# Issuing transposed strips from one queue, and writing out the order at the end of self attention, in a one-core Perceiver block

## The chip, the cores and the metric

The kernel runs on one core of one Trainium2 chip. Its metric is device time in microseconds, which is the time of one launch. In the profile the engines are PE (TensorE, matmuls; PEld is its weight load), DVE (VectorE), ACT (ScalarE), POOL (GpSimd) and SP (SyncE, which issues DMAs). A name with a q behind it (SPq, ACTq) is the engine's queue issuing a DMA.

## What is computed

The input is 8 rows of 128 tokens with 512 features, and 8 contexts of 2048 tokens with 384 features, all in float32. Cut to its core, the reference is:

```python
x = x + cross_attention(layernorm(x), ctx)  # 8 heads of 64, 2048 keys, then Wo and bo
x = x + self_attention(layernorm(x))        # 1 head of 512, causal mask, over 128 tokens
                                            # returns minibatch + read; softmax over axis 1
x = x + ffn(layernorm(x))                   # 512 -> 2048 (relu, rounded to e4m3), w2 rounded
                                            # to e4m3, -> 512, b2 and the output to e5m10
```

The "row" of this text is one of the 8 batch rows, a tile of 128 x 512.

## The kernel before

**Cross attention** is a loop over 8 batches `b`, and in it over 4 steps `m` of two heads each. In a step, `scores(b, m)` multiplies queries and keys (tile `sc`, line 568), and VectorE copies the products into the tile `p` with the maxima as a by-product (line 572). `p` lies in a pool with a single buffer. `exps` takes the exponential of both heads on ScalarE (line 586), after all maxima are there. `turns` transposes `p` in 32x32 blocks on VectorE (line 599), and 16 DMAs, the *strips* (line 605), move the blocks to their places in `pT`. In the next step, `attend` multiplies `pT` with the values (tile `po`, line 617). Between them TensorE works through a *unit*, which is one part of the next batch's key or value projection (lines 469 and 492). A unit is a generator: its results leave PSUM by copies on ScalarE (`take`) and additions on VectorE, and it yields three times, so that other instructions can be placed between its parts.

Of the strips, SyncE's queue gets the first 12 (`STRIPS[:-Q]`, `Q` is 4). The last four go to ScalarE's queue, behind the first two or three parts of the unit. In the last batch, from step 1 on, three queues share the 16.

**Row transfers** go from ScalarE's queue at the start of a step, right behind `scores` in program order. Step 1 has `load_u` (a constant line, line 658). Step 3 stores two tiles of the batch before (`xtd` and `xr`, lines 906 and 907) and loads the next row (`load_x`, line 654). SyncE's queue also carries the context loads of `next_half` (line 190, at steps 0 and 3) and `load_q` (line 550, at step 0).

**Self attention** is split into two groups of four rows, `sa0` and `sa1`. Their methods are `norm`, `turn` (transpose on TensorE, copy by ScalarE into `xt`), `keys` (`psk`, copied to `sk` by ScalarE), `weights` (logits `pl`, exponential), `probabilities`, `values` (`psv`) and `read` (`pr`). The first group runs inside the last batch's steps 1 to 3. The second comes after the loop, mixed with the last `attend` and the last two projects (`py`). Then the feed forward begins: `hidden` (`ph`), `output` (`pf`), and `quantize_w2`, which rounds `w2` in 16 chunks on ScalarE and VectorE.

**What sets the order.** Each engine's instructions of a `manual_schedule` block stand in the order of the program text. TensorE is under such a block through the whole kernel. ScalarE (`in_turn`) and VectorE (`first`) are so until `first.close()` and `in_turn.close()`. What is written after that is placed by a planner, and in the trace some of it stands between the instructions of the blocks (square roots of the feed forward's norms, rounding of `w2`). PSUM gives seven banks to all tiles that are made by `bank`.

Of the kernel before, what the change touches and what calls it, by code (L numbers as in the profile page):

```python
# [17 lines left out]
P = 128  # L18
# [49 lines left out]
def tile_perceiver_block(  # L68
# [75 lines left out]
    def normed(b, pool, tag, bufs, name, add_to=False):  # L144
        xn = pool.tile([P, D], F32, tag=tag, name=f"xn_{name}_{b}", bufs=bufs)
        normed_into(xn, b, name)
        if add_to:
            nc.gpsimd.tensor_tensor(xs[b], xs[b], xn, ALU.add)
        return xn
# [219 lines left out]
    wv_sums = wxa.tile([P, len(WSLOT), 256], F32, tag="wv_sums", name="wv_sums")  # L369
    sum_w(lambda k, j: wk4[:, k, :, j, :], wk_sums, nc.vector)  # L370

    kts, vts, ps_, sums, qts, turned_, pos, nms, wides = [{} for _ in range(9)]

    def block_product(name, mm, views, outs):

# [177 lines left out]
    def scores(b, m):  # L553

        q = qts[b][:, m, :]
        if m == 0:
            sums[b] = small.tile([P, NH], F32, tag="sums", name=f"sums_{b}")
        mx = small.tile([P, 2, NJ], F32, tag="mx", name=f"mx_{b}_{m}", bufs=3)  # L560

        home, tag = (ktp, "kt0") if (b, m) == (B - 1, 2) else (pp, "p")
        p = home.tile([P, Q, 2, J // Q], F32, tag=tag, name=f"p_{b}_{m}")
        for n in range(NJ):
            pair = [bank(f"sc_{b}_{2 * m + i}_{n}") for i in range(2)]
            for i in range(2):
                r = slice(i * DH, (i + 1) * DH)
                nc.tensor.matmul(  # L568
                    pair[i], q[r, :], kts[b, m // 2][r, m % 2, ts(n, 512)], start=True, stop=True
                )  # L570
            for i in range(2):
                nc.vector.tensor_scalar(  # L572
                    p[:, :, i].rearrange("p g (t i) -> p t g i", i=SQ)[:, ts(n, Q)],
                    pair[i].rearrange("p (t g i) -> p t g i", g=Q, i=SQ),
                    1.0, None, ALU.mult, ALU.max, accum_out=mx[:, i, n : n + 1],
                )
        top = small.tile([P, 2], F32, tag="top", name=f"top_{b}_{m}", bufs=3)
        nc.vector.reduce_max(top, mx, axis=AX.X)
        nm = small.tile([P, 2], F32, tag="nm", name=f"nm_{b}_{m}", bufs=3)
        nc.vector.tensor_scalar(nm, top, -SCALE, None, ALU.mult)  # L580
        ps_[b, m], nms[b, m] = p, nm

    def exps(b, m, i):

        p, h = ps_[b, m], 2 * m + i
        nc.scalar.activation(  # L586
            p[:, :, i], p[:, :, i], AF.Exp, bias=nms[b, m][:, i : i + 1], scale=SCALE,
            accum_out=sums[b][:, h : h + 1],
        )
# [137 lines left out]
    class SelfAttention:  # L727


        def __init__(self, g, pool, w):  # L730
# [6 lines left out]
            self.vals = pool.tile([P, GB, D], F32, tag="sv", name=f"sv_{g}")  # L737
            self.xn, self.es = {}, {}

        def norm(self, b):  # L740
            self.xn[b] = normed(b, self.pool, "xn", GB, "s", add_to=True)
            unread = self.pool.tile([P, D], BF16, tag="unread", name=f"unread_{b}")
            row_constant(b, self.xn[b], self.u, unread)

# [62 lines left out]
                self.values(r)  # L807
            yield

        def values_and_reads(self, rows):  # L810
            for r in rows:
                self.values(r)
            for r in self.rows:
                self.read(r)
            yield

        def read(self, b):
            ps = bank(f"pr_{b}")
# [75 lines left out]

    sa0 = None
    for b in range(B):
        last = b + 1 == B
        for m in range(NK):  # L900
            scores(b, m)

            if m == 1 and b > 0 and not last:
                load_u(b - 1)
            if m == 3 and b > 0 and not last:
                nc.scalar.dma_start(xtd[:, :, ts(b - 1, S)], stats[b - 1])
                nc.scalar.dma_start(xr[:, b - 1, :], xs[b - 1])
            if m == 3 and b < B - 2:
                load_x(b)
            unit = None  # L910
            if m > 0:
                attend(b, m - 1)
            elif b > 0:

                attend(b - 1, NK - 1)
            if m == 0:
                unit = v_proj(b, 1)
            elif not last and m == 1:
                unit = v_proj(b + 1, 0)
            elif not last:  # L920
                unit = k_proj(b + 1, m - 2)
            elif m == 1:
                unit = sa0.keys(sa0.rows)
            elif m == 2:
                unit = sa0.weights_and_values(sa0.rows[:3])
            else:
                unit = sa0.values_and_reads(sa0.rows[3:])
            if b == m == 0:

                keys = k_proj(0, 1, (1,))  # L930
                first_of(keys)
                first_of(keys)
                exps(b, m, 0)
                all_of(keys)
            else:
                exps(b, m, 0)
                if unit and not (last and m > 0):
                    first_of(unit)
            if m == 3 and last:
                bring_rows()  # L940
                for r in sa0.rows:
                    sa0.probabilities(r)
            exps(b, m, 1)
            if b == m == 0:
                all_of(both_weights())
            if m == 0 and b > 0:
                turned = normalized_first(b - 1)
                if last:
                    bring_last_rows()
            if m == 1 and b > 0 and not last:  # L950
                row_stats(b - 1)
            if m == 2 and b > 0 and not last:
                norm_rows(b - 1)
            strips = turns(b, m)
            if last and m > 0:

                strips([nc.sync, nc.gpsimd, nc.scalar], STRIPS)
            else:
                strips([nc.sync], STRIPS[:-Q])
            if m == 0 and b > 0:  # L960
                ot = normalized(b - 1, turned)
            if m == NK - 1:
                inverse_sums(b)
            if not (last and m > 0):

                for _ in range(3 if b == m == 0 else 2):
                    first_of(unit)
                strips([nc.scalar], STRIPS[-Q:])
            if unit:
                all_of(unit)  # L970
            if m == 1 and b > 0 and not last:
                row_scale(b - 1)
            if m == 3:
                next_half(b + 2, 0)
            if m == 0:
                next_half(b + 1, 1)
                if not last:
                    load_q(b + 1)
                if b > 0:
                    project(b - 1, ot)  # L980
                if last:
                    sap, w, sa0 = enter_self_attention()
    sa1 = SelfAttention(1, sap, w)
    sa1.norm(B - 2)
    for r in sa1.rows[:2]:
        sa1.values(r)
    sa1.turn(B - 2)
    attend(B - 1, NK - 1)
    ot = normalized(B - 1, normalized_first(B - 1))
    sa1.values(B - 2)  # L990
    xa.close()
    project(B - 1, ot)
    sa1.norm(B - 1)
    keys = first_of(sa1.keys(sa1.rows[:3]))

    sa1.turn(B - 1)
    all_of(keys)
    sa1.values(B - 1)
    all_of(sa1.keys(sa1.rows[3:]))
    first.close()  # L1000
    in_turn.close()

# [12 lines left out]
    def quantize_w2():  # L1015
        quantize(nc, tp, b2q, b2r, E5M10, "qb")
        for c in range(NHC):
# [2 lines left out]
            up = tp.tile([P, D], BF16, tag="w2c", name=f"w2c_{c}")  # L1020
            nc.scalar.activation(up, w, AF.Abs, scale=UP)
            round_e4m3(nc, tp, w2[:, c, :], w, up, "qw")

    def normed_rows(g, tag):
        xt = sap.tile([P, NK, GT], F32, tag=tag, name=f"xf_{g}")
        for b in range(g * GB, (g + 1) * GB):
            turned_into(xt, b, normed(b, sap, "xn", GB, "f"), "f")
        return xt

    hqs, firsts = {}, {}  # L1030

# [33 lines left out]

    def finish(b, ps, cols=slice(0, D), add=nc.gpsimd):
        n = cols.stop - cols.start
        y = sap.tile([P, n], F32, tag="xn", name=f"y_{b}_{cols.start}", bufs=GB)
        nc.vector.tensor_tensor(y, ps[:, cols], b2q[:, cols], ALU.add)  # L1069
        quantize(nc, tp, y, y, E5M10, "qb")  # L1070
        add.tensor_tensor(y, y, xs[b][:, cols], ALU.add)
        nc.sync.dma_start(out[b][:, cols], y)

    for r in sa1.rows:
        sa1.weights(r)
    for r in sa1.rows:
        sa1.probabilities(r)
    xf0 = normed_rows(0, "xt0")
    for r in sa1.rows:
        sa1.read(r)  # L1080
    quantize_w2()
    half, xfs = NHC // 2, [xf0]
    pairs = [range(b, b + 2) for b in range(0, B, 2)]
    hidden(pairs[0], xf0, range(0, NHC, 4))
    for i in range(1, len(pairs)):
        last = i + 1 == len(pairs)
        if i == 1:
            xfs.append(normed_rows(1, "xt1"))
        hidden(pairs[i], xfs[i // 2], range(0, half, 4))
        for b in pairs[i - 1]:  # L1090
            ps = bank(f"pf_{b}")
            output(b, ps, range(NHC))
            finish(b, ps)
        hidden(pairs[i], xfs[i // 2], range(half, NHC - 4 if last else NHC, 4))
# [58 lines left out]
```

## Time and profile before

| What | Value |
|---|---|
| Median of 3 runs | 1111.77 us (1110.84 to 1111.8) |
| The profiled execution | 1111.72 us |
| Its span, first to last instruction | 1109.9 us |
| TensorE clock granted | 0.998 |
| Cross attention's first `scores` | 84.26 us |
| Last `scores` of the loop | 899.56 us |
| First `ph` of the feed forward | 962.19 us |
| Last matmul | ends at 1098.99 us |

A line of the timeline has start, duration, engine, source line, operation, the written tile and the tiles read, and how many instructions it merges. In brackets stands the idle time ahead of it and what ended it. A line of the waits has the waiting engine and tile, what it waited for, the total, the number of times and the longest, in us.

### The profile page before, as it was taken

Reading aid. Unit: us, or ns where it says so; the run is one execution under the profiler, and the core shown is the slowest. Engines: PE = TensorE matmul, PEld = TensorE weight load, DVE = VectorE, ACT = ScalarE, POOL = GpSimd, SP = SyncE. Lnnn points to the kernel's source line nnn. Section 1 sums busy time; section 2 is a strip of 40 time slices with the busy share of each in tenths; the row PEclk is TensorE's granted clock in tenths of the full one; section 3 lists DMA queues with packets and bytes.
Section 4 is the critical chain, followed back from the end, with each engine's and each line's share of the span. In section 5 each row is a group of like instructions: output and inputs, shape, how many; then the busy total and the mean of one; then the engine's idle time right before and its main releaser. Section 6 shows DMA issues by size and latency. Waiting matters only on the chain. (4 is left out here: it accounts for less than half of the span.)

```text
span 1109.9 us, 17006 instructions
## 1 busy us (share of the span) xinstructions
PE 1096.2 (99%) x6286; PEld 830.7 (75%) x6286; DVE 811.0 (73%) x1736; ACT 381.8 (34%) x627; POOL 239.2 (22%) x349
## 2 busy tenths in 40 slices
PE   9999999999999999999999999999999999999997
PEld 5485888878787777878788878887777645787775
DVE  5975577778777776877787777777876575986656
ACT  3322233324233323333243324233323322663332
POOL 0244130440044005401520450044001011000001
PEclk9999999999999999999999999999999999999999
DMA  9376234544455445344534554555436457400001
GB/s 324 130 190 166 91 77 109 156 136 100 124 147 142 105 116 170 77 114 134 142 76 115 154 139 99 134 155 130 104 77 186 137 162 246 112 3 20 16 4 39
DMA packets 71859, 134.85 MB, mean 121 GB/s; under 512 B 28240, under 2 KB 36448, under 8 KB 70752
## 3 DMA queue, kind: packets, MB, share of 16 engines
q1 hardware_dynamic: 55264, 97.03, 32.5%
q10 hardware_dynamic: 13632, 26.88, 8.8%
q0 software_dynamic: 2880, 9.85, 2.7%
q8 instruction: 50, 0.82, 0.3%
q14 instruction: 33, 0.27, 0.1%
HBM read 54.01 MB, written 10.49 MB: 58 GB/s over the span
## 5 line engine op out<-in xcount | busy, mean ns | idle before, releaser
L586 ACT ACTIVATE p<-p,nm 128x2048 f32<-128x2048 f32 x64 | 128.2, 2003 | 411.9 <-DVE nm L580 370.6
L599 DVE STREAM_TRANSPOSE p<-p 128x512 f32<-128x512 f32 x256 | 158.9, 679 | 61.1 <-ACT p L586 60.8
L572 DVE TENSOR_SCALAR_CACHE_REDUCE p<-sc 128x512 f32<-128x512 f32 x256 | 159.0, 687 | 28.5 <-PE sc L568 18.2
L229 POOL TENSOR_TENSOR m<-x 128x256 f32<-128x256 f32 x70 | 51.2, 732 | 500.5 <-DMA x<-in_ctx_t_dram 362.7
L492 PE MATMUL pv_z<-wv_sums,x 128*128 128x256 f32 x640 | 157.9, 381 | 0.0
L469 PE MATMUL pk_z<-x,wk_sums 128*128 128x256 f32 x600 | 149.9, 382 | 0.7 <-ACT kt L388 0.6
L492 PEld LDWEIGHTS pv_z<-wv_sums,x 128*128 128x128 f32 x640 | 120.4, 190 | 18.6 <-issue 2.9
L617 PEld LDWEIGHTS po<-pT,v 128*64 128x64 f32 x2048 | 111.1, 137 | 23.7 <-issue 22.1
L469 PEld LDWEIGHTS pk_z<-x,wk_sums 128*128 128x128 f32 x600 | 112.4, 190 | 20.4 <-DVE xn_s L681 1.0
L568 PE MATMUL sc<-kt,q 64*128 64x512 f32 x512 | 122.7, 603 | 1.0 <-DVE p L572 1.0
L617 PE MATMUL po<-pT,v 128*64 128x128 f32 x2048 | 118.9, 274 | 0.0
L1049 PE MATMUL ph<-xf,w 128*128 128x256 f32 x512 | 111.3, 379 | 0.0
L1049 PEld LDWEIGHTS ph<-xf,w 128*128 128x128 f32 x512 | 97.2, 190 | 13.9 <-issue 0.5
L492 PE MATMUL pv_z<-wv_sums,m 128*128 128x256 f32 x448 | 107.3, 379 | 0.0
L469 PE MATMUL pk_z<-m,wk_sums 128*128 128x256 f32 x420 | 101.4, 379 | 0.0
L568 PEld LDWEIGHTS sc<-kt,q 64*128 64x128 f32 x512 | 48.2, 186 | 63.4 <-issue 55.4
L492 PEld LDWEIGHTS pv_z<-wv_sums,m 128*128 128x128 f32 x448 | 83.4, 190 | 12.6 <-POOL x L229 0.6
L469 PEld LDWEIGHTS pk_z<-m,wk_sums 128*128 128x128 f32 x420 | 78.4, 190 | 11.8 <-DVE kt L391 0.4
L388 ACT COPY v<-pv_z 128x512 f32<-128x512 f32 x112 | 63.0, 590 | 56.7 <-PE pv_z L492 56.7
L388 ACT COPY kt<-pk_z 128x512 f32<-128x512 f32 (+1 forms) x112 | 59.9, 563 | 55.8 <-PE pk_z L469 55.4
L229 POOL TENSOR_TENSOR x<-x 128x256 f32<-128x256 f32 x98 | 70.2, 736 | 0.6 <-DMA x<-in_ctx_t_dram 0.5
L391 DVE TENSOR_TENSOR v<-pv_z,v 128x512 f32<-128x512 f32 x96 | 63.1, 685 | 5.5 <-PE pv_z L492 5.5
(200 smaller groups left out, 1258.1 us busy)
## 6 DMA issues: line engine op xcount, KB each, us to landing
pT<-p SPq DMA_DIRECT2D x366, 128.0 KB, 2.4
x<-in_ctx_t_dram SPq DMA_DIRECT2D x45, 512.0 KB, 5.6
pT<-p ACTq DMA_DIRECT2D x131, 128.0 KB, 3.0
w<-in_w_t_dram SPq DMA_DIRECT2D x1, 4096.0 KB, 13.8
w2f<-in_w_t_dram SPq DMA_DIRECT2D x16, 256.0 KB, 2.7
x_in<-in_x_dram SPq DMA_DIRECT2D x8, 256.0 KB, 7.0
qd<-xq SPq DMA_DIRECT2D x8, 256.0 KB, 2.5
q<-qd SPq DMA_DIRECT2D x8, 256.0 KB, 3.2
```

What stands on the lines that cost most here:

```text
L229: eng.tensor_tensor(x_block(b, h, to), x_block(b, h, one), x_block(b, h, two), ALU.add if op == "+" else ALU.subtract,)
L388: nc.scalar.copy(outs[ij], views(ps))
L391: nc.vector.tensor_tensor(outs[to], views(ps), outs[other], op)
L469: nc.tensor.matmul(ps[:, ts(i, BK)], wk_sums[:, WSLOT[WAT[r]], f2, :], x_block(b, h, XAT[r]), start=start and i == 0, stop=True, skip_grou ...
L492: nc.tensor.matmul(ps[:, ts(t, 256)], x[:, ts(t, P)], wv_sums[:, WSLOT[WAT[r]], :], start=start and t == 0, stop=True, skip_group_check=True,)
L568: nc.tensor.matmul(pair[i], q[r, :], kts[b, m // 2][r, m % 2, ts(n, 512)], start=True, stop=True)
L572: nc.vector.tensor_scalar(p[:, :, i].rearrange("p g (t i) -> p t g i", i=SQ)[:, ts(n, Q)], pair[i].rearrange("p (t g i) -> p t g i", g=Q, ...
L586: nc.scalar.activation(p[:, :, i], p[:, :, i], AF.Exp, bias=nms[b, m][:, i : i + 1], scale=SCALE, accum_out=sums[b][:, h : h + 1],)
L599: nc.vector.transpose(p[:, g, i], p[:, g, i])
L617: nc.tensor.matmul(pos[b][h * DH : (h + 1) * DH, ts(m, P)].rearrange("p (a i) -> p a i", a=Q), v[:, jt % 8, ts(2 * m + h, DH)], turned_[b, ...
L1049: nc.tensor.matmul(ps[:, :n], w1[:, k, ts(c, P)], xt[:, k, at], start=(k == 0), stop=(k == NK - 1),)
```

## The change

It has two parts.

First, the strips of regular steps: all 16 now go to SyncE's queue, and the four on ScalarE's are gone. A new function `after_strips` puts a small copy on ScalarE at steps 1 and 3, ahead of the row transfers. The copy reads one of the maxima that VectorE makes with its first copy of the new `p`.

Second, the end of self attention. `norm` is split into `stats` (VectorE), `scale` (square root on ScalarE) and the rest. The values of the fourth row of `sa0` and its reads move out of step 3 to behind the loop. The norms of the feed forward's first four rows, an exponential of a constant (`warm`), the second group's weights, probabilities and reads, and the transposes of the feed forward's first group now stand inside the written order, with the last row's weights and probabilities behind those of the three rows before it. The blocks are closed after that.

```diff
-        ps_[b, m], nms[b, m] = p, nm
+        ps_[b, m], nms[b, m], mxs[b, m] = p, nm, mx
+    def after_strips(b, m):
+        seen = small.tile([P, 1], F32, tag="seen", name=f"seen_{b}_{m}")
+        nc.scalar.copy(seen, mxs[b, m][:, 0, 0:1])
...
+        def stats(self, b):
+            st = small.tile([P, 6], F32, tag="st", name=f"st_s_{b}", bufs=4)
+            nc.vector.bn_stats(st, xs[b])
+            mv = small.tile([P, 2], F32, tag="mv", name=f"mv_s_{b}", bufs=4)
+            nc.vector.bn_aggr(mv, st)
+            self.xn[b] = (mv,)
+        def scale(self, b):
+            sd = small.tile([P, 1], F32, tag="sd", name=f"sd_s_{b}", bufs=4)
+            nc.scalar.activation(sd, self.xn[b][0][:, 1:2], AF.Sqrt, bias=eps)
+            self.xn[b] += (sd,)
         def norm(self, b):
-            self.xn[b] = normed(b, self.pool, "xn", GB, "s", add_to=True)
+            mv, sd = self.xn[b]
+            rs = small.tile([P, 1], F32, tag="rs", name=f"rs_s_{b}", bufs=4)
+            nc.vector.reciprocal(rs, sd)
+            self.xn[b] = self.pool.tile([P, D], F32, tag="xn", name=f"xn_s_{b}", bufs=GB + 2)
+            nc.vector.tensor_scalar(self.xn[b], xs[b], mv[:, 0:1], rs, ALU.subtract, ALU.mult)
+            nc.gpsimd.tensor_tensor(xs[b], xs[b], self.xn[b], ALU.add)
             unread = self.pool.tile([P, D], BF16, tag="unread", name=f"unread_{b}")
             row_constant(b, self.xn[b], self.u, unread)
...
+    def turned_rows(g, rows, tag):
+        xt = sap.tile([P, NK, GT], F32, tag=tag, name=f"xf_{g}")
+        for i, xn in enumerate(rows):
+            turned_into(xt, g * GB + i, xn, "f")
+        return xt
...
             scores(b, m)
+            if m % 2 and not last:
+                after_strips(b, m)
             if m == 1 and b > 0 and not last:
                 load_u(b - 1)
...
             else:
-                unit = sa0.values_and_reads(sa0.rows[3:])
+                sa1 = SelfAttention(1, sap, w)
...
                 for r in sa0.rows:
                     sa0.probabilities(r)
+                sa1.stats(B - 2)
             exps(b, m, 1)
+            if m == 3 and last:
+                sa1.scale(B - 2)
...
             else:
-                strips([nc.sync], STRIPS[:-Q])
+                strips([nc.sync], STRIPS)
...
-            if not (last and m > 0):
-                for _ in range(3 if b == m == 0 else 2):
-                    first_of(unit)
-                strips([nc.scalar], STRIPS[-Q:])
             if unit:
                 all_of(unit)
...
-    sa1 = SelfAttention(1, sap, w)
+    sa0.values(sa0.rows[-1])
     sa1.norm(B - 2)
     for r in sa1.rows[:2]:
         sa1.values(r)
+    sa0.reads()
     sa1.turn(B - 2)
     attend(B - 1, NK - 1)
     ot = normalized(B - 1, normalized_first(B - 1))
     sa1.values(B - 2)
     xa.close()
     project(B - 1, ot)
+    sa1.stats(B - 1)
+    sa1.scale(B - 1)
     sa1.norm(B - 1)
+    xf0 = [normed(b, sap, "xn", GB + 2, "f") for b in range(GB)]
+    nc.scalar.activation(warm, eps, AF.Exp)
     keys = first_of(sa1.keys(sa1.rows[:3]))
     sa1.turn(B - 1)
     all_of(keys)
     sa1.values(B - 1)
+    for r in sa1.rows[:3]:
+        sa1.weights(r)
+    for r in sa1.rows[:3]:
+        sa1.probabilities(r)
     all_of(sa1.keys(sa1.rows[3:]))
+    sa1.weights(B - 1)
+    xfs = [turned_rows(0, xf0, "xt0")]
+    sa1.probabilities(B - 1)
+    sa1.reads()
     first.close()
     in_turn.close()
...
-    for r in sa1.rows:
-        sa1.weights(r)
-    for r in sa1.rows:
-        sa1.probabilities(r)
-    xf0 = normed_rows(0, "xt0")
-    for r in sa1.rows:
-        sa1.read(r)
     quantize_w2()
```

The feed forward's second group of norms and transposes keeps its place and is written with the new helper; the tiles `xn` and `y` get six buffers instead of four.

More of the change, by code (lines that the diff above doesn't have):

```diff
@@ L370, in tile_perceiver_block @@
     sum_w(lambda k, j: wk4[:, k, :, j, :], wk_sums, nc.vector)
-    kts, vts, ps_, sums, qts, turned_, pos, nms, wides = [{} for _ in range(9)]
+    kts, vts, ps_, sums, qts, turned_, pos, nms, wides, mxs = [
+        {} for _ in range(10)
+    ]
     def block_product(name, mm, views, outs):
@@ L808, in weights_and_values, with reads @@
             yield
-        def values_and_reads(self, rows):
-            for r in rows:
-                self.values(r)
+        def reads(self):
             for r in self.rows:
                 self.read(r)
-            yield
         def read(self, b):
@@ L1022, in quantize_w2 @@
             round_e4m3(nc, tp, w2[:, c, :], w, up, "qw")
[L1024 to L1028, printed above, removed]
     hqs, firsts = {}, {}
@@ L1067, in finish @@
         n = cols.stop - cols.start
-        y = sap.tile([P, n], F32, tag="xn", name=f"y_{b}_{cols.start}", bufs=GB)
+        y = sap.tile([P, n], F32, tag="xn", name=f"y_{b}_{cols.start}", bufs=GB + 2)
         nc.vector.tensor_tensor(y, ps[:, cols], b2q[:, cols], ALU.add)
@@ L1072, in finish @@
         nc.sync.dma_start(out[b][:, cols], y)
-    for r in sa1.rows:
-        sa1.weights(r)
-    for r in sa1.rows:
-        sa1.probabilities(r)
-    xf0 = normed_rows(0, "xt0")
-    for r in sa1.rows:
-        sa1.read(r)
     quantize_w2()
-    half, xfs = NHC // 2, [xf0]
+    half = NHC // 2
     pairs = [range(b, b + 2) for b in range(0, B, 2)]
-    hidden(pairs[0], xf0, range(0, NHC, 4))
+    hidden(pairs[0], xfs[0], range(0, NHC, 4))
     for i in range(1, len(pairs)):
@@ L1087, in tile_perceiver_block @@
         if i == 1:
-            xfs.append(normed_rows(1, "xt1"))
+            rows = [normed(b, sap, "xn", GB + 2, "f") for b in range(GB, B)]
+            xfs.append(turned_rows(1, rows, "xt1"))
         hidden(pairs[i], xfs[i // 2], range(0, half, 4))
```

## The prediction

> **What bounds the kernel now.** I read the page's first part first, then TensorE's waits, then the timeline at the places where they fall.
>
> ```profile
> PE 1096.2 (99%) x6286; PEld 830.7 (75%) x6286; DVE 811.0 (73%) x1736; ACT 381.8 (34%) x627; POOL 239.2 (22%) x349
> ```
>
> TensorE is busy for 1096.2 of 1109.9 us. It starts at 1.46 and its last matmul ends at 1098.99; the 11 us behind that are the last row's rounding and store, which the change leaves alone. Neither version adds or drops a matmul. So the change is worth what it takes from, or adds to, TensorE's stalls, and these are short. All waits of TensorE:
>
> ```profile
> PE pr L819 <- DVE e L791: 1.7, 1, 1.7
> PE early L279 <- POOL ident masks.py:199: 1.5, 1, 1.5
> PE pr L819 <- DVE sv L801: 1.2, 1, 1.2
> PE sc L568 <- DVE p L572: 1.0, 2, 0.6
> ```
>
> The two on `pr` (2.9 us) lie at the end of self attention. The third, on `sc`, is larger than it looks, because ends of matmuls are modelled and a stall can be counted as busy. I measure it from the start of `sc` to the start of the `po` behind it:
>
> ```profile
> 570.69 3.70 PE L568 MATMUL sc<-kt,q 64*128 64x512 f32 x16
> 574.33 0.88 PE L617 MATMUL po<-pT,v 128*64 128x128 f32 x12
> ...
> 595.88 4.41 PE L568 MATMUL sc<-kt,q 64*128 64x512 f32 x16
> 600.22 1.97 PE L617 MATMUL po<-pT,v 128*64 128x128 f32 x32
> ```
>
> The first pair, step 2 of batch 4, takes 3.64 us, as nearly all do. The second, step 3, takes 4.34. The steps 3 of batches 1 to 6 take 5.31, 4.45, 5.19, 4.34, 4.06 and 3.64: 5.15 us too much in sum. Before each, VectorE waits for strips (waits of VectorE, then the same place in the timeline):
>
> ```profile
> DVE p L572 <- DMA pT<-p: 10.3, 5, 2.7
> ```
>
> ```profile
> 588.77 2.37 ACTq L605 DMA_DIRECT2D pT<-p  x3
> 589.02 3.87 SPq L605 DMA_DIRECT2D pT<-p  x2
> 591.34 0.59 ACTq L906 DMA_DIRECT2D xtd<-xt_s  x1
> 591.97 0.66 ACTq L907 DMA_DIRECT2D xr<-x  x1
> ```
>
> `p` has one buffer, so the next scores can't be written until all 16 strips have read it. The SP strip that starts at 589.02 is followed by the next only at 592.39. The ACT strip of 588.77 needs 3.60 us to land: 592.37. I take it that the SP strip waits for that ACT strip (they would share a completion semaphore). The ACT strips themselves wait for copies of projection banks. Then three row transfers start on top, and the last SP strips land in 3.8 to 4.7 us; the last at 598.17, and VectorE starts at 598.41, 1.4 us later than its usual 1.16 after `sc`.
>
> **What the skill says.** "DMA: Bandwidth & Descriptors", section "Issuing engines are not separate DMA queues": all queues feed the same 16 DMA engines and a second issuer saves only issue time. The trace agrees: alone, SP's first seven strips of 662.64 take 4.32 us to issue and land in 2.4 us; with ACT beside it landings grow to 3 to 4.7. "ScalarE: Activation LUTs", section "What ACT_TABLE_LOAD costs": 1283 ns and a drain of 1380. The trace has 1.28 us, and no such drain (955.62 to the exponential at 956.91), so I use 1.28. "SBUF — State Buffer", section "Who interferes with whom": a GpSimd read can block a VectorE instruction with two SBUF inputs. The trace fits: `c_rows` took 1.10 us at 921.26 while GpSimd added rows, 0.15 at 939.70.
>
> **Part 1, strips and row transfers.** SP issues four more strips, ACT four fewer. Undisturbed strips on SP start 0.634 us apart (the median of intervals 2 to 8) and land in 2.35, so 16 take 15 x 0.634 + 2.35 = 11.9 us from the first issue. In the trace's semaphore records eight are used in turn; after eight issues (5.1 us) the earlier strip has long landed. Nearest evidence for so long a run: the last 16 `turned_w` strips of half the size, 0.67 us apart. Today's runs take 11.1 (step 3, 609.29 to 620.41), 12.3 to 12.9 (steps 0 and 1) and 14.8 (step 2, 583.39 to 598.17). VectorE wants `p` 13.2 us after the first issue at steps 1 and 3 (244.64 to 257.87), 13.6 at step 2, and TensorE stands a further 0.66: VectorE starts 1.16 behind `sc` as a rule, 2.25 cost 0.42 and 2.53 cost 0.70, so losses begin at 1.82. So 11.9 clears every step by 1.3 us and all 5.15 us go. Behind SP's strips are the context loads (`L190`), which at step 3 wait until 621.03 for TensorE's last read, after the 16th strip's issue at 619.4; at step 0 they start no later than now.
>
> The hold is a 128x1 copy on ACT that waits for the first maxima. Behind it in ACT's queue are one or three DMA issues (0.4 to 0.66 us each) and the exponentials, which need all maxima, about 4.5 us later: 0.2 + 1.9 us fit in. ACT waited 370.6 us in sum for those maxima. The rows are wanted a step or more (25 us) later. I take nothing for all this; without the cover it is at most some 0.5 us a step. **Sum: -5.2** (bounds -6 and -3).
>
> **Part 2a, self attention, before the last attention.** Before: row 3's values, four reads with the 1.21 us stall, values of two rows, `pt_s`, `po` at 922.68. After: values of three rows, then reads; their inputs are then ready, and TensorE reaches `po` at 921.2 or so. But the last strips of (7, 3) landed only at about 922.1 (three queues, landings of up to 6.8 us), and `sa1.stats`, 0.9 us on VectorE where it had 0.6 idle ahead of the transposes, moves them by 0.2 to 0.3. So the stall of 1.2 turns into one of 1.1 at `po`: **-0.2** (bounds -1.2 and +0.4).
>
> **Part 2b, after the last project.** Let 0 be the start of `psk`. TensorE before:
>
> ```profile
> 933.68 5.32 PE L757 MATMUL psk<-xt,both 128*128 128x384 f32 x16
> 938.84 0.60 PE L155 MATMUL pt_s<-ident,xn_s 128*128 128x128 f32 x4
> 939.28 5.33 PE L757 MATMUL psk<-xt,both 128*128 128x384 f32 x16
> 944.44 3.60 PE L797 MATMUL psv<-swv,xt 128*128 128x512 f32 x8
> ```
>
> `psv` of row 7 starts at 10.8 and reads `xt`, which ACT copies out of `pt_s` (939.52 before). After, with ACT in program order, that copy stands behind four square roots, a table load, and two `sk`. VectorE's order ahead of it: add of the projection, 0.2 to 0.9; statistics, root, reciprocal, norm to 2.9; `unread` and constant to 3.8. Then four rows, each `bn_stats` 0.69, `bn_aggr` 0.18, root 0.29, reciprocal 0.16, norm 0.46 (the next overlaps it), with 0.03 to 0.04 at each hand-over: 1.93. The fourth root ends at 3.8 + 3 x 1.93 + 1.2 = 10.8. Then the load 1.28 and `warm` 0.25, two `sk` 1.1, the copy 0.6: 14.05. TensorE waits 3.3 us where it waited for nothing. GpSimd's add beside `c_rows` (up to 0.9) and roundings of `w2` that fill VectorE's gaps (0.6 each) lengthen it: I take 3.8 (bounds 2.5 and 6). Afterwards the 1.73 us at `pr` go: the exponentials of three rows lie three steps ahead, and behind row 7's logits stand `pt_f` (1.75) and three reads (2.6), against 2.9 from logits to probabilities. **Sum: 3.8 - 1.7 = +2.1.**
>
> **Part 2c, feed forward.** VectorE was full from 934 to 962 (27.89 of 28) and had rounded about half of `w2` by then; from 962 to 1005 it has 8 us free (35.01 of 43). If it starts 2 or 3 chunks (1.9 us each) later, those 8 us hold them. Cost 0; bound +3, if ACT then waits for `h` buffers longer than the 6 us that seven banks give TensorE.
>
> **Sum.** -5.2 - 0.2 + 2.1 = -3.3. The profiled execution took 1111.72 us (span 1109.9, 1.8 around it), so 1108.4; the median of the runs, 1111.77, is the same to 0.05.
>
> **Rivals.** (1) Forecast: 1108.4, by itself 1107.0 to 1110.0. (2) The new wait at `psv` doesn't come or is under 1 us, because the roots finish while `psk` runs, and both old stalls go: -5.2 - 2.9 + 0.5 = -7.6, 1104.1. For it: TensorE gives 10.8 us of cover; against it: the chain of single hand-overs above. (3) Slower: a single queue is the limit. If SP's strips start more than (13.2 + 0.66 - 2.35) / 15 = 0.77 us apart, the last lands late at each of some 20 steps; at 0.80, 0.46 us each, 9 us, so 1111.7 + 9.2 - 3.3 = 1117.6. For it: with ACT beside it the average spacing is 0.80 to 0.93; against: those averages hold the wait for ACT's strips. (4) The late strips at step 2 have another cause and stay, the rest comes as I say: 1111.7 + 1.9 = 1113.6; the ordering (transfers at 591 to 593, late strips right after) speaks against it.
>
> Chances: forecast 0.5, (2) 0.2, (3) 0.12, (4) 0.18. A difference under 0.2% (2.2 us) isn't told from none here. Faster: (2) and most of the forecast, 0.63; same: the rest of it and part of (4), 0.2; slower 0.17. The range 1103.5 to 1114.0 holds the first two cases and more than half of (4).
>
> **What will show it.** All `sc` groups at 3.64 to the next `po`; no VectorE wait for `pT`; 16 strips on SP 0.63 us apart, done within 12 us of the first. A wait of `psv` on ACT's `xt` copy of 3 to 4 us after the last `py`, a short one of `po` on the strips, none on `pr`. I am wrong if strip spacing exceeds 0.77, if `psv` doesn't wait, or if `ph` or `pf` begin to.

## The result, and the profile after

| | before | after |
|---|---|---|
| Median of 5 runs each | 1111.77 us (1110.84 to 1111.96) | 1115.9 us (1115.14 to 1117.74) |
| Ratio | | 1.0042 [1.0028, 1.0057] |
| The profiled execution | 1111.72 us | 1115.14 us |
| Its span | 1109.9 us | 1113.4 us |
| TensorE clock granted | 0.998 | 0.996 |
| Last `scores` of the loop start | 899.56 us | 893.57 us |
| From there to its `po` | 23.12 us | 24.58 us |
| From `po` to the first `ph` | 39.51 us | 47.48 us |
| From `ph` to the end | 147.7 us | 147.7 us |

The changed kernel is 0.4% slower. The lower four lines are times in the two profiled executions, and their differences, -6.0, +1.5, +8.0 and 0.0, are the +3.5 us between the spans. The loop gave what was forecast; all that was lost lies in the 72 us between the last `scores` and the feed forward. In both kernels the last matmul ends some 7.5 us ahead of the end; before, that is at 1102.47 us, and not at 1098.99 as the table of the time before and the prediction have it.

First the loop. These are TensorE's groups at the place that the prediction shows, step 3 of batch 4, from the timeline of the kernel after:

```profile
591.02 3.70 PE L570 MATMUL sc<-kt,q 64*128 64x512 f32 x16
594.65 2.62 PE L625 MATMUL po<-pT,v 128*64 128x128 f32 x43
```

From `sc` to `po` are now 3.63 us instead of 4.34, and no group of the loop takes longer. Ahead of it, the DMA issues of the same stretch:

```profile
578.53 10.44 SPq L613 DMA_DIRECT2D pT<-p  x16
...
592.97 0.54 ACTq L937 DMA_DIRECT2D xtd<-xt_s  x1
...
593.55 0.63 ACTq L938 DMA_DIRECT2D xr<-x  x1
```

The 16 strips are issued in a row and have landed at 590.74, 12.2 us behind the first. Only then, at 592.97, does the first row transfer follow. Before, the strips took 14.8 us and the transfers stood in their midst.

Now the end. All waits of TensorE of half a microsecond or more, by total, times and longest, but for two in the first 100 us that both kernels have:

```profile
PE psv L822 <- ACT xt L156: 7.0, 1, 7.0
PE po L625 <- DMA pT<-p: 2.9, 1, 2.9
...
PE pl L797 <- ACT sk L786: 0.6, 1, 0.6
```

The waits of `pr` are gone, as is that of `sc`. A wait of `psv` of 7.0 us and one of `po` of 2.9 have come. The timeline of TensorE there:

```profile
934.76 5.33 PE L782 MATMUL psk<-xt,both 128*128 128x384 f32 x16
947.11 5.52 PE L822 MATMUL psv<-swv,xt 128*128 128x512 f32 x8 [7.03 <-ACT xt L156]
952.47 2.84 PE L797 MATMUL pl<-xt,sk 128*128 128x128 f32 x24
```

The reader should look at two numbers of the middle line. Behind the bracket's 7.03 stands a duration of 5.52, for eight matmuls that took 3.60 before. The same stretch in windows (start:end and length in us, TensorE's busy time in it, granted clock, DMA share, GB/s) says why:

```profile
940.00:947.00 7.00, 0.08 (x1) 0.78 0.25 83
947.00:948.00 1.00, 0.89 (x1) 0.50 0.65 205
948.00:949.00 1.00, 1.00 (x3) 0.50 0.00 0
...
951.00:952.00 1.00, 1.00 (x3) 1.00 0.43 160
```

While TensorE waited, its clock was halved (granted clock 0.50), 3.9 us into the gap; it stayed so from 943.99 for 6.83 us. The first matmuls behind the gap run at half speed, which adds 1.92 us to the wait itself (5.36 instead of 3.44 from `psv` to the next group).

What `psv` waited for is seen in ScalarE's timeline:

```profile
936.30 0.29 ACT L139 ACTIVATE sd_f<-mv_f,eps 128x1 f32<-128x1 f32 x1 [4.56 <-DVE mv_f L137]
...
940.28 0.29 ACT L139 ACTIVATE sd_f<-mv_f,eps 128x1 f32<-128x1 f32 x1 [0.43 <-DVE mv_f L137]
943.31 0.63 ACT L1064 ACTIVATE w2c<-w2f 128x512 bf16<-128x512 f32 x1 [2.74 <-DVE w L63]
943.85 0.28 ACT L139 ACTIVATE sd_f<-mv_f,eps 128x1 f32<-128x1 f32 x1
944.14 1.28 ACT L1028 ACT_TABLE_LOAD   x1
...
945.55 1.03 ACT L786 ACTIVATE sk<-psk,side 128x384 f32<-128x384 f32 x2
946.47 0.58 ACT L156 COPY xt<-pt_s 128x512 f32<-128x512 f32 x1
```

The order is the one the prediction gave: the roots (`sd_f`, the first and the last two of the four are shown), the load, two `sk`, the copy. But from the third root to the fourth are 3.57 us, not 1.93, and in them stands a `w2c`, which is rounding of `w2` that the planner put there. VectorE's side, further ahead, has the same for `b2`:

```profile
929.97 0.42 DVE L39 TENSOR_SCALAR qb_e<-b2r 128x512 int32<-128x512 int32 x1
930.30 0.69 DVE L750 BATCH_NORM_STATS2 st_s<-rows 128x6 f32<-128x512 f32 x1
930.90 0.41 DVE L40 TENSOR_SCALAR qb_e<-qb_e 128x512 f32<-128x512 f32 x1
931.23 0.17 DVE L752 BATCH_NORM_AGGREGATE mv_s<-st_s 128x2 f32<-128x6 f32 x1
...
933.48 1.76 DVE L702 SCALAR_TENSOR_TENSOR unread<-xn_s,u 128x512 bf16<-128x512 f32 x1
```

Each step of row 7's norm has an instruction of `b2`'s rounding (`qb`) in front of it.

### The profile page after: what moved, and what is told of

It is laid out like the page before. It is cut to its first block, busy times and chain, and to the rows that moved or that the text cites. A ratio compares the mean times of both kernels' runs of the same rounds, so it can differ in the third digit from the quotient of the medians.

```text
span 1113.4 us, 17022 instructions
## 1 busy us (share of the span) xinstructions
PE 1093.3 (98%) x6286; PEld 830.0 (75%) x6286; DVE 812.0 (73%) x1736; ACT 383.7 (34%) x642; POOL 239.1 (21%) x349
## 4 chain that ended last, share of the span: by engine, by line
PE 94%; DVE 4%; ACT 1%; DMA 1%; issue 0%; ACTq 0%; POOL 0%; DVEq 0%; POOLq 0%
PE pv_z L494 21%; PE pk_z L471 20%; PE sc L570 10%; PE po L625 10%; PE ph L1086 10%; PE pv_b L494 4%; PE pk_b L471 3%; PE py L708 2%; PE pq L538 2%; PE pf L1098 2%; PE k L453 2%; PE psk L782 1%; PE psv L822 1%; PE pw L357 1%; DMA pT<-p 1%
## 5 line engine op out<-in xcount | busy, mean ns | idle before, releaser
L570 PE MATMUL sc<-kt,q 64*128 64x512 f32 x512 | 118.5, 602 | 0.0
```

What stands on the lines that cost most here:

```text
L570: nc.tensor.matmul(pair[i], q[r, :], kts[b, m // 2][r, m % 2, ts(n, 512)], start=True, stop=True)
```

## The experiments

The theory after the result: part 1 does what was forecast, and the end lost by the new wait of `psv`, lengthened by rounding that was placed in its chain, and by the clock that fell behind it. The rivals: the loop's gain or loss is elsewhere; the wait comes from the written order alone; the late strips of the last step are the larger part. Ratios are against the kernel before; durations at single places are those of the profiled execution of each.

### The two parts, each by itself

Part 1 in the kernel before (strips and `after_strips`, no change of the end):

```diff
+            if m % 2 and not last:
+                after_strips(b, m)
...
-                strips([nc.sync], STRIPS[:-Q])
+                strips([nc.sync], STRIPS)
...
-                strips([nc.scalar], STRIPS[-Q:])
```

> The kernel before with part 1 alone. Theory A (the two parts are independent, the loss is all at the end of self attention): the sc groups of steps 3 fall to 3.64 us to the next po, some 5.2 us less than before, so about 1106.5 us (ratio 0.9953); the waits of pr stay at 1.7 and 1.2. Rival B (strips from one queue make something else late, such as the context loads, and the end only shows it): less than 3 us gained, over 1109.

Measured: 1105.89 us (1105.68 to 1106.8), ratio 0.9949 [0.9937, 0.9962]. The `sc` wait is gone, the two of `pr` (1.7 and 1.2) are there as before.

Part 2 alone, which is the kernel after with the strips put back on two queues, and no hold:

> The changed kernel with part 1 taken back (12 strips on SP, 4 on ACT, no hold). Theory A: it keeps before's late strips and has the whole loss of the end, 1115.9 + 5.2 to 6, so about 1121 us (ratio 1.009), with psv waiting about 7 us for ACT's xt copy. Rival B: about 1112 to 1116.

Measured: 1121.87 us (1121.1 to 1123.71), ratio 1.0094 [1.008, 1.0108]. The waits of `psv` (7.0) and `po` (2.8) are those of the kernel after, and the clock is halved at the same place for 6.83 us. So part 1 is worth -5.9 us and part 2 +10.1. Their sum, +4.2, is the +4.1 of the whole.

### Which half of part 1 gives it

The strips moved, without the hold:

```diff
-                strips([nc.sync], STRIPS[:-Q])
+                strips([nc.sync], STRIPS)
...
-                strips([nc.scalar], STRIPS[-Q:])
```

> The kernel before with 16 strips on SP and no hold of the row transfers. Theory A (the late strips at step 2 come from SP's ninth strip waiting for an ACT strip, and the row transfers start only behind ACT's strips because they share its queue): without ACT's strips the row transfers start right at the beginning of step 3 or earlier, among the strips; a part of the gain is lost: 1106 to 1109 us. Rival E (the hold does nothing): 1105.9 as with part 1.

The hold, with the strips left on two queues:

```diff
             scores(b, m)
+            if m % 2 and not last:
+                after_strips(b, m)
```

> The kernel before with the hold of the row transfers and the strips as they were (12 on SP, 4 on ACT). Theory A (the SP strips are late by their wait for ACT's strips, some 3 us, and by the row transfers on top, some 1.5 us, each enough for a part of the 5.2 us): half or more of the gain, 1107 to 1109.5 us. Rival F (the wait for ACT's strips alone does it): 1111 to 1112, no gain.

The move alone: 1112.38 us (1110.94 to 1114.22), ratio 1.0003 [0.9994, 1.0011]. The hold alone: 1106.46 (1105.71 to 1106.88), 0.9947 [0.9934, 0.9959]. The hold is the whole gain; the move gains nothing by itself, and nothing that can be told from the spread of the runs on top of the hold (1105.89 with both). The DMA issues ahead of the same step 3, first with the move alone, then with the hold alone:

```profile
581.42 13.64 SPq L612 DMA_DIRECT2D pT<-p  x16
...
586.25 0.54 ACTq L913 DMA_DIRECT2D xtd<-xt_s  x1
...
586.83 0.85 ACTq L914 DMA_DIRECT2D xr<-x  x1
```

```profile
578.57 10.29 SPq L612 DMA_DIRECT2D pT<-p  x12
...
583.39 2.72 ACTq L612 DMA_DIRECT2D pT<-p  x4
...
592.94 0.19 ACT L588 COPY seen<-mx 128x1 f32<-128x1 f32 x1 [8.97 <-DVE p L574]
593.00 0.59 ACTq L915 DMA_DIRECT2D xtd<-xt_s  x1
```

Without the four strips in front of them the row transfers only start earlier, 4.8 us behind the first strip. The strips then take 15.4 us to land, which is longer than before (14.8). With the hold they take 12.0, though ACT still issues four of them. The waits of SP's own queue, over the whole kernel, name it (what was waited for, us in total, times, longest): before, with the move alone, and with the hold alone.

```profile
SPq L605 <- DMA pT<-p: 100.1, 51, 5.1
```

```profile
SPq L612 <- DMA pT<-p: 27.8, 20, 6.2
...
SPq L612 <- DMA xtd<-xt_s: 12.5, 6, 2.3
SPq L612 <- DMA u<-line: 11.6, 6, 2.7
```

```profile
SPq L612 <- DMA pT<-p: 92.5, 48, 5.4
```

With the move alone, SP's strips wait for row transfers that another queue has issued: at the step shown 2.1, 0.7 and 0.6 us for the three of them, together as much as the 3.4 us that the strips land later than with the hold. Before, it was another mix: at this step SP's queue waited 3.2 us for strips, instead of 2.2 with the hold alone, and the last strip, issued among the transfers, needed 3.8 us to land instead of 2.3. With the hold alone the strips still wait 92.5 us for strips over the whole kernel, nearly as long as before, and it costs TensorE nothing. Summed over the loop, the groups of `sc` are 5.15 us too long before, 5.3 with the move alone, and none is too long with the hold alone. The Trainium skill ("DMA: Bandwidth & Descriptors", section "Issuing engines are not separate DMA queues") says that a second issuer saves only the time of issuing; these runs agree. Nor is it ACT's strips alone that make landings longer, as the prediction read it: in the kernel after, where SP issues alone, the fourth to the seventh of these 16 strips still need 3.0 to 3.9 us. What counts is whether the row transfers stand among the strips, not who issues the strips.

### What lengthens the wait of `psv`

The feed forward's four norms behind the last row's transpose, and `warm` behind the keys:

```diff
-    xf0 = [normed(b, sap, "xn", GB + 2, "f") for b in range(GB)]
-    nc.scalar.activation(warm, eps, AF.Exp)
     keys = first_of(sa1.keys(sa1.rows[:3]))
     sa1.turn(B - 1)
+    xf0 = [normed(b, sap, "xn", GB + 2, "f") for b in range(GB)]
     all_of(keys)
+    nc.scalar.activation(warm, eps, AF.Exp)
```

> The changed kernel with the four norms of the feed forward moved behind the turn of the last row, and the exponential of the constant behind the last sk copies, so that the xt copy stands ahead of the four square roots on ACT. Theory A: the wait of psv on xt goes (7.0 us) and with it the half clock behind it (1.9 us), so about 1107.5 us (ratio 0.996); the clock share rises from 0.996 to 0.998. Rival C (the chain on VectorE is long anyway and only moves): pl or pr wait in its place for several us, over 1111 us.

Measured: 1110.85 us (1108.84 to 1112.9), ratio 0.9994 [0.9986, 1.0003]. The `psv` wait is gone, and so is 5 us of the time. More was expected. TensorE's timeline shows where it stayed:

```profile
918.30 5.21 PE L625 MATMUL po<-pT,v 128*64 128x128 f32 x64 [2.43 <-DMA pT<-p]
...
947.44 3.97 PE L797 MATMUL pl<-xt,sk 128*128 128x128 f32 x20 [1.83 <-ACT sk L786]
```

`po` takes 5.21 us for 64 matmuls that take 3.71 in the kernel after, and the clock is halved from 918.0 for 3.41 us; the gap ahead was 2.43. The logits (`pl`) wait 1.83, because `sk` now stands behind the roots, and the clock is halved again from 948.72 for 3.41. The runs of this kernel differ from each other more than those of the other kernels, and their times go with the mean granted clock of each: 1108.84 to 1109.14 us in the three runs at 0.998, 1111.91 to 1112.9 in the five at 0.995. The profiled one is of the latter. A mean of 0.998 is what the kernels without such a fall have, so the falls seen in the trace are not in every run.

All rounding of `w2` and `b2` in written order behind the reads:

```diff
     sa1.reads()
-    first.close()
-    in_turn.close()
...
     quantize_w2()
+    first.close()
+    in_turn.close()
```

> The changed kernel with the rounding of w2 and b2 inside the written order, so that none of it can stand between the norms. Theory A, if the prediction's sum of the chain was right but for what fills VectorE's gaps: psv waits 3.3 to 4.4 us instead of 7.0, and too short a gap for the clock to fall, if the clock falls only behind long ones (it fell 4.1 us into the gap). The time itself then depends on how the rounding crowds the feed forward: 1111 us if that costs nothing, more if ph or pf wait. Rival D (the chain itself is slower than summed): psv waits 6 us or more as before.

Measured: 1120.52 us (1119.75 to 1121.49), ratio 1.008 [1.0067, 1.0092]. The wait of `psv` is close to what the prediction had taken. A new one is larger:

```profile
PE pf L1096 <- DVE w L64: 5.9, 3, 3.8
PE psv L822 <- ACT xt L156: 3.9, 1, 3.9
```

So the chain of written instructions is worth 3.9 us, and the 3.1 above it come from rounding placed in it. ScalarE's first and fourth root in this kernel tell where:

```profile
934.88 0.29 ACT L139 ACTIVATE sd_f<-mv_f,eps 128x1 f32<-128x1 f32 x1 [3.50 <-DVE mv_f L137]
...
940.78 0.29 ACT L139 ACTIVATE sd_f<-mv_f,eps 128x1 f32<-128x1 f32 x1 [1.69 <-DVE mv_f L137]
```

Between them lie 5.90 us, and 7.55 in the kernel after (936.30 to 943.85), where nothing but `w2` is rounded in that stretch. So about 1.6 of the 3.1 us are rounding of `w2` between the roots, and the other 1.5, ahead of the first root, are that of `b2` in row 7's norm. But rounded as late as here, `w2` isn't there when `pf` wants it, and the clock is halved behind that wait too, from 1012.05 for 6.83 us. The gaps it fills at the end of self attention are needed.

The loads of `b2` and `b1` behind that of `w1` on SP, so that they leave GpSimd's queue:

```diff
-    b2r = load_row(wff, b2, "b2r")
...
+    nc.sync.dma_start(b2r, b2.partition_broadcast(P))
...
+    nc.sync.dma_start(b1c, b1)
```

> The changed kernel with the loads of b2 and b1 on SP behind w1 instead of on GpSimd's queue. Theory A (GpSimd's row addition comes earlier than before, and so b2's load starts in the middle of the last strips and takes 1.3 us of the DMA engines from them): the last strip lands some 11 us after the first issue instead of 12.2, po waits 1.3 to 1.8 us instead of 2.9, and b2's five roundings leave the chain ahead of xt, so psv waits 5.5 to 6 us instead of 7.0: about 1113 us. Rival D (the strips are slow for another reason): po still waits 2.8 to 2.9.

Measured: 1112.24 us (1110.8 to 1113.07), ratio 0.9998 [0.999, 1.0007]. The waits:

```profile
PE psv L822 <- ACT xt L156: 4.6, 1, 4.6
PE po L625 <- DMA pT<-p: 1.6, 1, 1.6
```

`b2` arrives too late to be rounded in row 7's norm, and 2.4 of the 3.1 us go from `psv`: the 1.5 ahead of the first root, and about 1 between the roots, where `w2` and now `b2` too are rounded (6.56 us from the first to the fourth). That `po` waits 1.2 us less shows what had held its strips up. GpSimd's timeline of the kernel after:

```profile
909.34 1.60 POOL L766 TENSOR_TENSOR rows<-rows,xn_s 128x512 f32<-128x512 f32 x1
910.89 0.58 POOL L727 DMA_DIRECT2D b2r<-in_b_dram  x1
```

The load of `b2` (256 KB), and behind it that of `b1` (8 KB), stand behind the addition of a row. Before, the addition came at 920.58, and so the load at 922.29, behind all strips. With row 6's norm earlier, it goes out among the strips of the last step, whose landing ends 12.2 us behind their first issue; with the load moved, 10.95, and before, 10.7. The other traces bear this out: 11.7 to 12.2 us in the four kernels with the load of `b2` among these strips, 10.3 to 11.5 in the eight without.

### Mending the end

On top of the moved loads, and keeping the last row ordered as in the kernel after: the feed forward's first four norms share one square root and stand ahead of the last `attend`, so that nothing but row 7 is left in the chain of `psv`; and row 6's values are split in two, half of them ahead of `attend`, to give the strips time. The reads of the first group stand one row earlier.

```diff
-    for r in sa1.rows[:2]:
-        sa1.values(r)
+    sa1.values(sa1.rows[0])
     sa0.reads()
     sa1.turn(B - 2)
+    sa1.values(sa1.rows[1])
+    rs = normalized_first(B - 1)
+    xf0 = normed_together(range(GB))
+    two = first_of(sa1.values_in_two(B - 2))
     attend(B - 1, NK - 1)
+    next(two)
...
-    xf0 = [normed(b, sap, "xn", GB + 2, "f") for b in range(GB)]
     nc.scalar.activation(warm, eps, AF.Exp)
```

> The changed kernel with b2 and b1 behind w1, and another order at the end: reads of the first group right behind its last values, the four norms of the feed forward together with one square root ahead of the last attention, half of row 6's values ahead of it and half behind. Nothing else is changed. Theory A: no wait of TensorE over 1 us is left at the end, the clock doesn't fall; against part 1 alone (1105.9) the two waits of pr (2.9 us) are gone: 1102.5 to 1104 us (ratio 0.992 to 0.993). Rival C (the roundings of w2 fill VectorE whatever the order and something waits for them): pl, pr or pf wait, 1105 us or more.

Measured: 1111.36 us (1110.19 to 1112.49), ratio 0.9994 [0.9986, 1.0002]. The end of self attention is clean, and the first `ph` comes at 953.79, while it comes at 956.46 with part 1 alone. Yet part 1 alone is 5.5 us faster as a whole. TensorE's timeline behind `ph`:

```profile
986.34 1.05 PE L155 MATMUL pt_f<-ident,xn_f 128*128 128x128 f32 x4 [2.08 <-DVE xn_f L142]
988.39 1.09 PE L155 MATMUL pt_f<-ident,xn_f 128*128 128x128 f32 x4 [1.00 <-DVE xn_f L142]
```

The feed forward's second group of norms is now late. VectorE has the same rounding to do in less time (five chunks of `w2` are done ahead of the first `ph`, where the kernel before had seven), and the norms come in between. Four waits of 0.6 to 2.1 us follow each other, and then the clock is halved from 986.39 for 6.83 us.

So those four norms go into the written order as well, right behind the reads:

```diff
     sa1.reads()
+    xf1 = normed_together(range(GB, B))
     first.close()
...
-            rows = [normed(b, sap, "xn", GB + 2, "f") for b in range(GB, B)]
-            xfs.append(turned_rows(1, rows, "xt1"))
+            xfs.append(turned_rows(1, xf1, "xt1"))
```

> The mended order, and the norms of the feed forward's second four rows together, with one square root, in the written order right behind the last reads. Theory G (the end is now clean, and what was left in the mended order was pt_f of the second group waiting for norms that the planner had put behind roundings on a full VectorE, 4.5 us, with half the clock behind it, 2 us): the waits of pt_f go, 1104 to 1105.5 us (ratio 0.993). Rival C (VectorE's sum of work up to the first pf is the bound, so the stall only moves to ph or pf): 1107 us or more.

Measured: 1103.74 us (1103.58 to 1104.52), ratio 0.9928 [0.9915, 0.9942]. It beats both kernels, and part 1 alone by 2.15 us. Of TensorE's waits of half a microsecond or more two are left, both in the first 100 us:

```profile
PE early L279 <- POOL ident masks.py:199: 1.5, 1, 1.5
PE pk_z L471 <- ACT kt L390: 0.6, 1, 0.6
```

One more variant loads and rounds `b2` behind all 16 chunks of `w2`, with the load of `b1` back on GpSimd's queue.

> The same, with b2 loaded and rounded behind the 16 chunks of w2, and b1 back on GpSimd's queue. Theory G: the w2 loads come 0.5 us earlier and 2.5 us of rounding leave the full stretch of VectorE, which costs or gains under 1 us: 1103.5 to 1105.5 us. Rival C: a gain of over 1 us against the run before, as VectorE is the bound.

Measured: 1103.84 us (1103.21 to 1104.27), ratio 0.9927 [0.9914, 0.9939], no different from the one above. Once no wait of TensorE hangs on VectorE, it doesn't matter where `b2` is rounded.

## Why the prediction was wrong

Forecast was 1108.4 us, with 1103.5 to 1114.0 as the range; it took 1115.9. The step that failed is the sum of part 2b, the stretch behind the last project: +2.1 us were forecast, and +7.8 came. Its allowance for what is placed in the chain of `psv` was too small by 3.1 us, and the clock behind the wait stood at nothing without a reason. Part 2a failed too, by 1.7 us. The terms, beside what the profiled executions show:

| Term, as the prediction named it | Forecast | Measured |
|---|---|---|
| Part 1, strips and row transfers | -5.2 | -6.0 |
| Part 2a, ahead of the last attention | -0.2 | +1.5 |
| Part 2b, wait of `psv` | +3.8 | +7.0 |
| Part 2b, clock behind that wait | none | +1.9 |
| Part 2b, wait of `pl` | none | +0.6 |
| Part 2b, wait of `pr` that goes | -1.7 | -1.7 |
| Part 2c, feed forward | 0 | 0.0 |

The table leaves 0.2 us of the stretch to `ph` unassigned.

- **Part 1: right in size, wrong in cause.** All 5.15 us went; at the step shown the strips are 0.63 us apart and done in 12.2 us, at other steps in up to 13.5 (14.5 at the very first) without a wait of `sc`. The other 0.8 us lie ahead of the first `scores`. That start scatters from 83.3 to 84.7 us over the twelve traces, in no order that follows the edits, so they are no gain of the change. But the prediction gave the gain to the strips that SP no longer has to share with ACT, and let the hold cost and gain nothing. The single halves showed the reverse: by its own account of the cause the forecast would have failed without the hold (1112.38 us), so that its size came true is luck. The row transfers were in its fence, and it named them as coming "on top"; with them held back all of the loss went. Rival 3 (a single queue is the limit) is refuted by the spacing and by `sc` without waits, and rival 4 (late strips that stay) by the `sc` groups.
- **Part 2a: the strips' own landing failed.** The prediction took their time from before and moved it by 0.2 to 0.3 us. In fact that time grew by 1.5, and 1.2 of that went when the load of `b2`, which stands behind the norm's addition on GpSimd's queue, was moved. It had looked at what the moved norm does to VectorE, and not at what stands behind its addition on GpSimd. With the load moved, the wait falls from 2.9 to 1.6, where 1.1 had been forecast.
- **Part 2b: the mechanism was right, two terms failed.** The wait came at the named place with the named releaser, and the chain by itself is 3.9 us (3.3 by the sum, 3.8 as taken). The first term that failed is the half microsecond allowed for GpSimd's addition and the rounding together. The addition used it up: with rounding in order `c_rows` takes 1.10 us beside it, and the chain came 0.6 us above the sum. The rounding came on top with 3.1 us, 1.5 of `b2` and 1.6 of `w2`. The Trainium skill ("SBUF — State Buffer", section "Who interferes with whom") says that an instruction with two SBUF inputs contends with a GpSimd instruction that reads; the traces agree, and they show that it makes 0.1 of the 3.1 us at most. In the kernel after, GpSimd's addition starts 0.17 us ahead of `unread`, which takes 1.76 us, and `c_rows` behind it 0.16; with rounding in order `unread` starts 0.05 us ahead of the addition and takes 0.69, and `c_rows` 1.10. The two together take 1.96 and 1.83 us. The second term is the clock: the price of the wait was set at its length, and the 1.9 us of half clock behind it were missing in the sum.
- **Rival 2** (the wait doesn't come) is refuted by the waits. The prediction sought a slower case only at the strips, so the one that came had no place among its rivals, and its upper bound for the wait of `psv`, 6 us, was too low.
- **Part 2c** was right for this kernel, by the equal time from `ph` to the end. Its worry came true only where the end got shorter (the mended kernel) or the rounding later (rounding in order).

## What to carry to other kernels

When a copy is moved behind other instructions of its engine, sum the chain of hand-overs, and then add every independent instruction that may be placed in its gaps on the engines it passes; they are short one by one, and here they made 7.0 us of a wait of 3.9. Look on every queue at what stands behind the instruction that is moved: a load that starts earlier can land among transfers that are needed first, and holding back transfers that nobody wants yet (one small copy ahead of them) was the whole gain of part 1. A wait of TensorE of a few us can cost more than its length, by the clock behind it (next section), and a stall that is removed at one place can come back where the same engine's work has been squeezed.

## What the runs showed of the hardware

TensorE's granted clock is full or half in these traces, and within one execution its changes lie on a grid of 3.413 us. With the norms behind they come at 918.00, 921.42, 948.72 and 952.13, which are 1, 8 and 1 steps apart; with rounding in order at 943.78, 947.19, 1012.05 and 1018.87, which are 1, 19 and 2 steps. This agrees with the Trainium skill ("TensorE: Matmul & The Clock Gate", section "What's actually happening"), which describes a free-running window of 3413 ns. So each gap of TensorE can be cut at the lines of the grid, and what lies idle inside one window can be set beside the clock of the next:

| Kernel | Gap ahead of | us | Most idle in one window | Half clock |
|---|---|---|---|---|
| before | `pr` | 1.73 | 1.73 | none |
| after | `po` | 2.87 | 1.47 | none |
| after | `psv` | 7.03 | 3.41 | 943.99, for 6.83 us |
| norms behind | `po` | 2.43 | 2.13 | 918.00, for 3.41 us |
| norms behind | `pl` | 1.83 | 1.83 | 948.72, for 3.41 us |
| rounding in order | `po` | 2.8 | 1.74 | none |
| rounding in order | `psv` | 3.92 | 3.41 | 943.78, for 3.41 us |
| rounding in order | `pf` | 3.84, with 0.62 ahead | 3.38 | 1012.05, for 6.83 us |
| loads moved | `po` | 1.64 | 1.64 | none |
| loads moved | `psv` | 4.58 | 2.84 | 942.88, for 6.83 us |
| mended | `pt_f` | 2.08 and 1.00, with 0.6 and 0.8 ahead | 2.73 (two gaps together) | 986.39, for 6.83 us |

The windows around `po`, first in the kernel after, then with the norms behind:

```profile
913.27:916.68 3.41, 2.01 (x8) 1.00 0.90 204
916.68:920.10 3.42, 1.95 (x36) 1.00 0.01 4
```

```profile
914.59:918.00 3.41, 1.28 (x6) 1.00 0.66 149
918.00:921.42 3.42, 3.12 (x30) 0.50 0.00 0
```

The gap of 2.87 us is cut in two by the grid, 1.40 and 1.47, and the clock stays; the shorter one of 2.43 lies with 2.13 in one window, and the next window has half clock. In all twelve traces, up to the last matmul, every window at full clock with 1.83 us idle or more was followed by half clock, and none with 1.74 or less was. The one case that doesn't fit lies in the window in which the last matmul of the kernel after ends (1.93 us idle, full clock behind it). At half clock a window with 0.29 us idle or less brought the full clock back, and one with 1.00 or more did not. The border between these figures is not measured, nor whether it is the same in other kernels.

The Trainium skill's section "HAM oscillation — how this bites in real kernels" on the same page puts the rule as no idle gaps over about 3.4 us. Here gaps of 2.43 and 1.83 us were enough, where they fell into one window. The price beyond the gap is half of what TensorE is busy at half clock: an estimate from the windows gives 1.56 us for `po` with the norms behind (half of 3.12), and 1.50 was measured (5.21 instead of 3.71); for `psv` in the kernel after it gives 1.86 (half of 0.29 and 3.42), and 1.92 was measured.

Only one execution of each kernel has a trace, and the lines of the grid lie elsewhere in each, as the falls at 943.99, 943.78 and 942.88 show. So the same gap can be cut in one run and not in the next. That fits the runs of the kernel with the norms behind, whose times go with their mean clock, and those of the kernel after: 1115.14 us at 0.996 in the profiled run, 1117.74 at 0.993 in the slowest.
